# A four-layer graph network on one core: leaner neighbour lists, earlier loads of x, earlier fused weights, small first groups

## The chip, the core and the metric

One core of a Trainium2 chip runs the whole program. The metric is the device time of one execution in microseconds (us), lower being better. The kernel before takes 1764.37 us (median of three runs, 1763.55 to 1769.72). The engines are named as in the profile: PE multiplies matrices (PEld is its weight load), DVE works on vectors, ACT applies functions and copies, POOL issues the gathers and small fills, SP issues the other transfers.

## What is computed

`x` has 3327 rows of 512 numbers, and `adj` is a 3327 x 3327 matrix of zeros and ones, sparse and densest in its first rows and columns. Each of four layers computes an update from the rows that `adj` selects, adds it to `x` and normalizes each row:

```python
x = _layernorm(x + L0(x, adj, W, a1, a2))       # attention, 8 heads of 64, elu
x = _layernorm(x + L1(x, adj, ...))             # mean of all neighbours, two linear maps, relu
x = _layernorm(x + L2(x, adj, ..., 64))         # mean of the first 64 neighbours, two linear maps
x = _layernorm(x + L3(x, adj, W, a))            # attention, 4 heads of 128, elu
```

## The kernel before

**Blocks and lists.** The rows are cut into 26 blocks of 128. Block 0, the densest, is worked as a dense block. For each of the other 25 the kernel builds, on the chip, a list of its neighbours (`structure`, L863): the block of `adj` is loaded in two halves (L877, SP), ACT turns it into a 0/1 mask and adds up each row (L884), DVE multiplies the mask by column codes (L899) and draws the codes out by MAX8 and MATCH_REPLACE8 (L912 to L929). Then the per-row lists are packed into one list per block: counts go through two small matmuls that sum over the rows before (L934, L935), ACT and DVE turn the four resulting columns into start positions, negated positions and midpoints (L937 to L943), a matmul takes differences (L946), and for each run of up to ten 128-place chunks ACT makes step functions (`u`, L956), PE multiplies (L963), ACT copies out (`vc`, L966) and DVE picks indices (L971 to L984). A list is filled from the front (near columns) and from its end (far columns), so each block has one or two near runs and one far run, each worked by itself. Tiles of the pool `mid` have one buffer each, so a list's step waits for the same step of the list before.

**Prologue.** Up to L1680, 26 projections run (L1597): load a block of x, transpose it (L783), multiply by the layer-0 weights `w0` (L1048, sixteen 268-column fp32 matmuls), copy out (L1059, L1060) and store the row to the table `t0_d` that layer 0 gathers from. Before them the score columns of `w0` are made on DVE (`score_weights`, L1545 to L1548) from `a0`, which is loaded after `w0`. With each projection the list generator makes three steps (`more(3)`, L1669). `fused_weights` (L1606), begun with t = 13, multiplies the layer-1 weights together: for each of eight rows of blocks a load, four transposes, eight 512-column fp32 matmuls (L800), one copy (L1623), and at the end a bias product of 16 matmuls (L1628). One step of it is taken per projection; what is left is done by `fused.drain()` (L1680), after `g0.head` and `g0.finish` (L1678), the latter giving the last table rows. `first_rows` begins with t = 10; its scan (L1643) and the fused weights use parts of the big tile `rows`, which in the profile is called gt and which later holds the gathered rows.

**Layers.** Layers 0 to 3 take the lists in groups of up to four chunks (`groups`, L988): POOL issues one indirect gather per chunk (L1010) into a ring, and PE multiplies the gathered rows by selection matrices (L1367 in layers 0 and 3, L1844 in layers 1 and 2). `groups` has an argument `first`, the sizes of the first groups; layer 3 calls it with (1, 2), the others without. Layer 0 goes on building lists (`more(1 + k % 2)`, L1763).

**Order.** Up to layer 0's end the order of instructions on each engine is that of an automatic scheduler, which takes ready instructions by program position. After that (`manual_schedule`) it is program order. [...]

Of the kernel before, what the change touches and what calls it, by code (L numbers as in the profile page):

```python
# [8 lines left out]
F32 = mybir.dt.float32  # L9
BF16 = mybir.dt.bfloat16  # L10
# [6 lines left out]
I16 = mybir.dt.int16  # L17
# [614 lines left out]
def sparse_path(ctx, tc, flag_i, x, adj, l0_w, l0_a1, l0_a2, l1_w_self, l1_b_self, l1_w_nb, l1_b_nb,  # L632
# [67 lines left out]
    dgs = keep.tile([P, NL, 2], F32, name="dgs")  # L700
    starts = keep.tile([P, NL, 2], F32, name="starts")
    nmids = keep.tile([P, NL, 2], F32, name="nmids")
    for l in (l for ls in lists for l in ls):
        l.nmid = nmids[:, l.at]
    half = keep.tile([P, 2, NB], F32, name="half")
# [46 lines left out]
    point5 = const.tile([P, 1], F32, name="point5")  # L752
    nc.gpsimd.memset(point5, 0.5)

# [108 lines left out]
    def structure(big, mid, ps, m0):  # L863
# [26 lines left out]
        for k, b in enumerate(order):  # L890
# [7 lines left out]
            for s in range(2):  # L898
                nc.vector.tensor_mul(val[:, s * HW:(s + 1) * HW], ms[s], code[:, s * HW:(s + 1) * HW])  # L899
            nc.vector.tensor_reduce(dgs[:, b - 1, 1:2], ms[0][:, :P], AX.X, ALU.add)  # L900
            pc = ps.tile([P, 8, P], BF16, name="lp")
            nc.tensor.transpose(pc[:, 0, :], ms[0][:, :P], ident16)
            nc.scalar.activation(col0[:, b, :], pc[:, 0, :], AF.Identity, saturate=False)
            for l in lists[b]:
                L, K, cuts, a = l.L, l.K, l.cuts, l.at
                dg = dgs[:, a, 0:1]
                nc.vector.tensor_scalar(dg, half[:, 0, b:b + 1], half[:, 1, b:b + 1], 1.0, ALU.add, ALU.max)
                nc.vector.tensor_sub(dg, dg, dgs[:, a, 1:2])
                n = len(cuts) - 1
# [7 lines left out]
                cf = cand.rearrange("p s e -> p (s e)")  # L917
                sl = mid.tile([P, K + 2], F32, name="sl")
                slots = sl[:, 2:]
                for r in range(K // 8):  # L920
# [15 lines left out]
                here = mid.tile([P, 2], F32, name="here")  # L936
                nc.scalar.activation(here[:, 0:1], p1[:, 0:1], AF.Identity, bias=point5, scale=-1.0)  # L937
                nc.vector.tensor_scalar(here[:, 1:2], p1[:, 1:2], -1.0, l.room - 0.5, ALU.mult, ALU.add)
                nc.scalar.copy(starts[:, a], p1[:, 0:2])
                nc.scalar.copy(sl[:, 0:1], p1[:, 0:1])  # L940
                nc.vector.scalar_tensor_tensor(sl[:, 1:2], p1[:, 1:2], 1.0 - l.room, dg, ALU.add, ALU.subtract)
                nc.scalar.activation(l.nmid[:, 0:1], p1[:, 2:3], AF.Identity, bias=ones[:, 0:1])
                nc.vector.tensor_scalar(l.nmid[:, 1:2], p1[:, 3:4], -1.0, 1.0 - 2 * l.room, ALU.mult, ALU.add)  # L943
                yield None
                p2 = ps.tile([P, 512], F32, name="p2", tag="lp")
                nc.tensor.matmul(p2[:, :K + 2], step, sl, start=True, stop=True)  # L946
                dl = dls[a % 2]
# [3 lines left out]
                G = min(SPAN, 512 // W)  # L951
                spans = [(0, c0, l.up) for c0 in range(0, l.up, G)] + [(1, c0, L) for c0 in range(l.down, L, G)]
                for far, c0, end in spans:
                    g = min(G, end - c0)
                    u = mid.tile([P, g * P], BF16, name="u")
                    nc.scalar.activation(u, place[:, c0 * P:(c0 + g) * P], AF.Sign, bias=here[:, far:far + 1],  # L956
                                         scale=-1.0 if far else 1.0)
                    if not far:
                        yield None
                    pv = ps.tile([P, 512], F32, name="pv")  # L960
                    for c in range(g):
# [4 lines left out]
                    nc.scalar.copy(vc[:, :g * W], pv[:, :g * W])  # L966
                    if not far:
                        yield None
                    v = vc[:, :g * W].rearrange("p (c k) -> p c k", k=W)
                    off = mid.tile([P, g, 1], I16, name="off")  # L970
                    nc.vector.tensor_sub(off[:, :, 0], (npos if far else pos)[:, c0:c0 + g], v[:, :, 1 + far])  # L971
                    eq = mid.tile([P, g, K], I16, name="eq")
                    nc.vector.tensor_tensor(eq, slot[:, None, :K].to_broadcast([P, g, K]),
                                            off.to_broadcast([P, g, K]), ALU.is_equal)
                    nc.vector.tensor_mul(eq, eq, v[:, :, 3:])
                    hit = mid.tile([P, g], I16, name="hit")
                    with nc.allow_low_precision(reason="whole numbers below 4096"):
                        nc.vector.tensor_reduce(hit, eq, AX.X, ALU.add)
                    at = l.idx[:, c0:c0 + g]
                    if far:  # L980
                        nc.vector.tensor_tensor(at, at, hit, ALU.add)
                        continue
                    nc.vector.scalar_tensor_tensor(at, hit, P + 1.0, hit, ALU.is_gt, ALU.mult)
                    nc.vector.scalar_tensor_tensor(l.dst[:, c0:c0 + g], hit, P + 1.0, v[:, :, 0],  # L984
                                                   ALU.is_gt, ALU.mult)
            yield k
# [44 lines left out]
    class Gat:  # L1031
# [242 lines left out]
        def group(self, item, pools, accs, done, sall=None):  # L1274
# [22 lines left out]
            for t, k, q0, q1 in parts:  # L1297
                if q0 < q1:
                    o = t[:, q0 * P:q1 * P] if t is far else t[:, :(q1 - q0) * P]
                    nc.scalar.activation(o, place[:, (c0 + q0) * P:(c0 + q1) * P], AF.Abs,  # L1300
                                         bias=l.nmid[:, k:k + 1], scale=2.0)
            yield
# [271 lines left out]
    with ExitStack() as pro:  # L1574
# [15 lines left out]
        a0 = lent(2 * D).rearrange("p (s h o) -> p s h o", s=2, h=H0)  # L1590
        for s, src in enumerate((l0_a1, l0_a2)):
            nc.sync.dma_start(a0[:, s].rearrange("p h o -> p (h o)"), row(src, H0 * OUT0))
# [144 lines left out]
    def feed():  # L1737
# [3 lines left out]
        for n, b in enumerate(blocks):  # L1741
            if n == len(blocks) - DENSE - 2:
# [121 lines left out]
    with ExitStack() as lay:  # L1864
# [316 lines left out]
```

## Time and profile before

| what | us |
|---|---|
| median of the runs | 1764.37 |
| the profiled execution itself | 1764.85 |
| its span, first to last instruction | 1763.1 |
| first gather of layer 0 | 211.55 |
| first gather of layer 1 | 742.24 |
| first gather of layer 2 | 1133.15 |
| first gather of layer 3 | 1457.15 |

The profile has several views. The windows give, for each stretch of time, the busy time of each engine in us and its number of instructions in brackets, then PE's granted clock as a share of full speed, the share of time that the 16 transfer engines were busy, and GB/s. The groups give, for one line and shape, the count, the busy sum in us, the mean of one in ns, and the idle time of the engine just before them. The timeline lists instructions by start, with the idle time before and its releaser in square brackets. "x10" in a timeline row stands for ten instructions merged.

### The profile page before, as it was taken

What the parts mean: (1) busy time and instruction counts of PE and PEld (TensorE: products, weight loads), DVE (VectorE), ACT (ScalarE), POOL (GpSimd) and SP (SyncE); (2) the same over time, 40 slices, a digit from 0 to 9 for tenths busy, and PEclk for the clock granted to TensorE, in tenths of its full rate; (3) what the DMA queues carried; (4) which work ended last, traced back from release to release, by engine and by line L of the source; (5) the groups of instructions that cost most, each with busy time, mean ns of one, the idle gap of its engine ahead of it and who ended that gap; (6) DMA issues with size and microseconds to landing.
All of it is one profiled execution on the core that took longest, in us unless ns stands there. A gap on an engine that the chain in (4) does not pass through costs nothing.

```text
span 1763.1 us, 24351 instructions
## 1 busy us (share of the span) xinstructions
PE 1505.3 (85%) x7266; PEld 1002.5 (57%) x7266; DVE 1219.4 (69%) x3292; ACT 872.8 (50%) x2922; POOL 760.5 (43%) x909
## 2 busy tenths in 40 slices
PE   5979847889999989889999999856999973878885
PEld 4756536656666667445555554422666752767664
DVE  8989859988668788225656785537666542867897
ACT  5879645656657767312122121211444442556786
POOL 3000146555454620164444652266656206666640
PEclk9989878999999999889999999988999996979998
DMA  8787667666665542298988995387878416767761
GB/s 258 260 274 240 210 190 247 216 185 200 189 188 154 173 123 80 82 401 292 303 287 306 342 371 191 98 285 247 279 255 269 153 43 189 198 199 211 225 198 56
DMA packets 130401, 381.98 MB, mean 217 GB/s; under 512 B 22037, under 2 KB 36477, under 8 KB 130259
## 3 DMA queue, kind: packets, MB, share of 16 engines
q0 software_dynamic: 67696, 252.97, 45.2%
q1 hardware_dynamic: 62563, 127.35, 21.4%
q8 instruction: 60, 0.98, 0.2%
q14 instruction: 82, 0.67, 0.1%
HBM read 331.89 MB, written 48.37 MB: 216 GB/s over the span
## 4 chain that ended last, share of the span: by engine, by line
PE 57%; DVE 17%; ACT 9%; issue 7%; another core or an unknown queue 4%; DMA 3%; POOL 2%; SPq 0%; DVEq 0%; POOLq 0%; ACTq 0%
PE po L800 18%; PE acc L1367 10%; PE acc L1844 9%; PE po L1048 8%; PE pt L783 3%; DVE cand L912 2%; DVE gt L1348 2%; DVE gl L1348 1%; PE acc L1836 1%; DVE st L805 1%; PE acct L1477 1%; PE acc L1255 1%; ACT h L1518 1%; DVE e L1531 1%
## 5 line engine op out<-in xcount | busy, mean ns | idle before, releaser
L1010 POOL DMA_INDIRECT gt<-t_d,idx x201 | 204.0, 1015 | 369.0 <-DVE mx L1147 197.4
L1010 POOL DMA_INDIRECT gl<-t_d,idx x265 | 261.6, 987 | 185.7 <-issue 56.7
L1367 PE MATMUL acc<-gt,sel 128*128 128x264 f32 (+3 forms) x804 | 208.2, 404 | 3.4 <-issue 1.9
L800 PE MATMUL po<-wn,xt 128*128 128x512 f32 x416 | 197.5, 618 | 15.5 <-ACT xt L786 5.8
L1010 POOL DMA_INDIRECT gm<-t_d,idx x138 | 136.1, 986 | 132.7 <-PE acc L1844 79.1
L1367 PEld LDWEIGHTS acc<-gt,sel 128*128 128x128 f32 (+3 forms) x804 | 150.7, 197 | 41.0 <-issue 15.9
L1367 PE MATMUL acc<-gl,sel 128*128 128x260 f32 (+3 forms) x524 | 140.3, 412 | 14.5 <-issue 11.0
L800 PEld LDWEIGHTS po<-wn,xt 128*128 128x128 f32 x416 | 79.3, 197 | 101.8 <-issue 79.4
L1048 PE MATMUL po<-gt,xt 128*128 128x268 f32 x416 | 115.9, 424 | 15.2 <-ACT xt L790 10.9
L1348 DVE TENSOR_TENSOR gt<-gt,pg 128x1536 f32<-128x1536 f32 (+3 forms) x63 | 116.4, 1848 | 14.8 <-ACT sel L1343 12.5
L1367 PEld LDWEIGHTS acc<-gl,sel 128*128 128x128 f32 (+3 forms) x524 | 100.6, 202 | 34.7 <-issue 15.6
L1844 PE MATMUL acc<-gm,selr 128*128 128x512 f32 (+3 forms) x324 | 106.6, 452 | 5.5 <-DMA gm<-t_d,idx 5.1
L1010 POOL DMA_INDIRECT gk<-t_d,idx x65 | 67.4, 1037 | 95.5 <-DMA t_d<-mean 58.6
L912 DVE MAX8 cand<-val 128x8 f32<-128x464 uint16 (+32 forms) x184 | 107.8, 622 | 0.0
L1048 PE MATMUL po<-w,xt 128*128 128x262 f32 x416 | 98.7, 391 | 9.6 <-ACT xt L790 5.8
L786 ACT COPY xt<-pt 128x512 f32<-128x512 f32 x81 | 46.9, 587 | 119.3 <-PE pt L783 83.6
L1048 PEld LDWEIGHTS po<-gt,xt 128*128 128x128 f32 x416 | 78.6, 202 | 34.7 <-ACT xt L790 14.5
L1300 ACT ACTIVATE far<-place,nmids 128x384 int16<-128x384 int16 (+3 forms) x167 | 88.2, 544 | 13.8 <-DVE ds L1310 9.9
L1048 PEld LDWEIGHTS po<-w,xt 128*128 128x128 f32 x416 | 78.9, 192 | 27.3 <-ACT xt L790 10.0
L800 PE MATMUL po<-wx,xt 128*128 128x512 f32 x208 | 93.5, 594 | 0.0
L800 PE MATMUL po<-wl,xt 128*128 128x512 f32 x208 | 93.0, 592 | 0.0
L783 PE MATMUL pt<-s_ident,xres 128*128 128x128 f32 x500 | 78.8, 285 | 10.4 <-DVE xres L855 5.3
(377 smaller groups left out, 3268.5 us busy)
## 6 DMA issues: line engine op xcount, KB each, us to landing
ab<-in_adj_dram SPq DMA_DIRECT2D x25, 832.0 KB
ab<-in_adj_dram SPq DMA_DIRECT2D x25, 831.5 KB
t_d<-t SPq DMA_DIRECT2D x25, 512.0 KB
gm<-t_d POOLq DMA_DIRECT2D x23, 512.0 KB
t_d<-t SPq DMA_DIRECT2D x25, 384.0 KB
t_d<-tg SPq DMA_DIRECT2D x25, 264.0 KB
gd<-t_d SPq DMA_DIRECT2D x25, 264.0 KB
t_d<-tg SPq DMA_DIRECT2D x25, 260.0 KB
```

Source lines behind the costliest of these rows:

```text
L783: nc.tensor.transpose(pt[:, c, :], src[:, c * P:(c + 1) * P], ident)
L786: nc.scalar.copy(xt, pt)
L800: nc.tensor.matmul(po, xt[:, c, :], w[:, c], start=c == 0, stop=c == DC - 1)
L805: nc.vector.bn_stats(st, y)
L912: nc.vector.max(out=cand[:, s, :], in_=val[:, cuts[s]:cuts[s + 1]])
L1010: nc.gpsimd.indirect_dma_start(out=t[:m, c, :], out_offset=None, in_=table[:, :], in_offset=bass.IndirectOffsetOnAxis(ap=l.idx[:m, c0 + c: ...
L1048: nc.tensor.matmul(pw[s], xt[:, c, :], self.w[:, c, s, :], start=c == 0, stop=c == DC - 1)
L1255: nc.tensor.matmul(self.acc[h // hh][:, h % hh, :], wt[:m, h, :], G[:m, h, :], start=False, stop=False)
L1300: nc.scalar.activation(o, place[:, (c0 + q0) * P:(c0 + q1) * P], AF.Abs, bias=l.nmid[:, k:k + 1], scale=2.0)
L1348: nc.vector.tensor_mul(Gc[:, :, :OUT], Gc[:, :, :OUT], w[:, :g].rearrange("p c (h o) -> p (c h) o", o=1).to_broadcast([P, g * H, OUT]))
L1367: nc.tensor.matmul(accs[b][s], S[:m, c, :], G[:m, c, s * hh * M:(s + 1) * hh * M], start=at + c == 0, stop=last)
L1844: nc.tensor.matmul(accs[b], chosen, parts[:, k * D:(k + 1) * D], start=at + c + k == 0, stop=k == top and at + c == n - 1)
```

## The change

It has four parts.

1. **Lists.** The count of a row's ones in its first 128 columns comes from ACT (the mask of the first half is made in two ACTIVATEs, each with its own sum) and no longer from a reduction on DVE. The start positions, negations and constants come out of five small matmuls, two of them with constant rows that POOL fills per list (`rooms`: four memsets), and two ACT copies of four columns take them out; the three DVE and four ACT instructions L937 to L943 go. A far run that fits beside the last near run into ten chunks is worked with it: two `u` instructions, but one copy out, one comparison, one product, one reduction. By the sizes of the lists that holds for 22 of the 25 blocks, all but 3, 4 and 5.
2. **Loads.** `a0` is loaded ahead of `w0`; blocks 0 to 2 of x are loaded ahead of the first block of `adj`, and each projection loads the block three further on.
3. **Fused weights** begin with t = 8. At one step per projection all 17 steps then fall within the projections.
4. **First groups.** The first two groups of layers 0, 1 and 2 have one and two chunks.

The core of the diff:

```diff
-    starts = keep.tile([P, NL, 2], F32, name="starts")
-    nmids = keep.tile([P, NL, 2], F32, name="nmids")
+    sites = keep.tile([P, NL, 4], F32, name="sites")
+    starts = sites[:, :, :2]
...
+    for k, v in enumerate((0.5, -0.5, 0.0, 1.0, 0.0, 0.0, 1.0, 1.0)):
+        nc.gpsimd.memset(halves[:, k:k + 1], v)
...
-                nc.scalar.activation(m, ab[s], AF.Sign, accum_out=half[:, s, b:b + 1])
+                c0 = P if b and s == 0 else 0
+                if c0:
+                    nc.scalar.activation(m[:, :P], ab[s][:, :P], AF.Sign, accum_out=dgs[:, b - 1, 1:2])
+                nc.scalar.activation(m[:, c0:], ab[s][:, c0:], AF.Sign, accum_out=half[:, s, b:b + 1])
...
-            nc.vector.tensor_reduce(dgs[:, b - 1, 1:2], ms[0][:, :P], AX.X, ALU.add)
...
-                nc.vector.tensor_scalar(dg, half[:, 0, b:b + 1], half[:, 1, b:b + 1], 1.0, ALU.add, ALU.max)
-                nc.vector.tensor_sub(dg, dg, dgs[:, a, 1:2])
+                nc.vector.tensor_add(dg, half[:, 0, b:b + 1], half[:, 1, b:b + 1])
+                nc.vector.scalar_tensor_tensor(dg, dgs[:, a, 1:2], 0.0, dg, ALU.is_equal, ALU.max)
...
-                dg16 = mid.tile([P, 2], BF16, name="dg16")
-                nc.vector.tensor_copy(dg16, dgs[:, a])
+                dg16 = mid.tile([P, 3, 2], BF16, name="dg16")
+                nc.vector.tensor_mul(dg16, signs, dgs[:, a, None, :].to_broadcast([P, 3, 2]))
+                rooms = mid.tile([1, 8], BF16, name="rooms")
+                nc.gpsimd.memset(rooms, 0.0)
+                for c, v in ((1, l.room), (3, -l.room), (6, -2 * l.room)):
+                    nc.gpsimd.memset(rooms[:, c:c + 1], float(v))
                 p1 = ps.tile([P, 512], F32, name="p1", tag="lp")
-                nc.tensor.matmul(p1[:, 0:2], before, dg16, start=True, stop=True)
-                nc.tensor.matmul(p1[:, 2:4], middle, dg16, start=True, stop=True)
...
+                nc.tensor.matmul(p1[:, :8], ones16, halves, start=True, stop=False)
+                nc.tensor.matmul(p1[:, :8], ones16, rooms, start=False, stop=False)
+                d6 = dg16.rearrange("p k s -> p (k s)")
+                nc.tensor.matmul(p1[:, :6], before, d6, start=False, stop=False)
+                nc.tensor.matmul(p1[:, 3:4], ident16, d6[:, 0:1], start=False, stop=False)
+                nc.tensor.matmul(p1[:, 6:8], middle, d6[:, 1:3], start=False, stop=True)
+                nc.scalar.copy(sl[:, :4], p1[:, :4])
+                nc.scalar.copy(sites[:, a], p1[:, 4:8])
...
+                spans = [[(0, c0, min(G, l.up - c0))] for c0 in range(0, l.up, G)]
+                ends = [(1, c0, min(G, L - c0)) for c0 in range(l.down, L, G)]
+                if len(ends) == 1 and spans[-1][0][2] + ends[0][2] <= G:
+                    spans[-1].append(ends.pop())
...
+        a0 = lent(2 * D).rearrange("p (s h o) -> p s h o", s=2, h=H0)
+        for s, src in enumerate((l0_a1, l0_a2)):
+            nc.sync.dma_start(a0[:, s].rearrange("p h o -> p (h o)"), row(src, H0 * OUT0))
         for c in range(DC):
...
+        for b in range(3):
+            load(xres[b], x, b)
         next(made)
...
-            load(xres[b], x, b)
+            if b + 3 < NB:
+                load(xres[b + 3], x, b + 3)
...
-            if t == 13:
+            if t == 8:
                 fused.add(fused_weights())
...
-            for item in groups(pools[0], (b,), True):
+            for item in groups(pools[0], (b,), True, () if n else (1, 2)):
...
+    nc.vector.tensor_add(deg[:, 1:], deg[:, 1:], dgs[:, :, 1])
...
-        for item in groups(ring, weave):
+        for item in groups(ring, weave, first=(1, 2)):
...
-        nexts = groups(ring, weave)
+        nexts = groups(ring, weave, first=(1, 2))
```

More of the change, by code (lines that the diff above doesn't have):

```diff
@@ L700, in sparse_path @@
     dgs = keep.tile([P, NL, 2], F32, name="dgs")
-    starts = keep.tile([P, NL, 2], F32, name="starts")
-    nmids = keep.tile([P, NL, 2], F32, name="nmids")
+    sites = keep.tile([P, NL, 4], F32, name="sites")
+    starts = sites[:, :, :2]
     for l in (l for ls in lists for l in ls):
-        l.nmid = nmids[:, l.at]
+        l.nmid = [sites[:, l.at, 3:4], sites[:, l.at, 2:3]]
     half = keep.tile([P, 2, NB], F32, name="half")
@@ L751, in sparse_path @@
         nc.gpsimd.memset(dl[:, 1, 0:1], 0.0)
-    point5 = const.tile([P, 1], F32, name="point5")
-    nc.gpsimd.memset(point5, 0.5)
+    signs = const.tile([P, 3, 2], F32, name="signs")
+    nc.gpsimd.memset(signs, 1.0)
+    nc.gpsimd.memset(signs[:, 0], -1.0)
+    ones16 = const.tile([1, P], BF16, name="ones16")
+    nc.gpsimd.memset(ones16, 1.0)
+    halves = const.tile([1, 8], BF16, name="halves")
+    for k, v in enumerate((0.5, -0.5, 0.0, 1.0, 0.0, 0.0, 1.0, 1.0)):
+        nc.gpsimd.memset(halves[:, k:k + 1], v)
     H0, _, OUT0 = l0_w.shape
@@ L917, in structure @@
                 cf = cand.rearrange("p s e -> p (s e)")
-                sl = mid.tile([P, K + 2], F32, name="sl")
-                slots = sl[:, 2:]
+                sl = mid.tile([P, K + 4], F32, name="sl")
+                here, slots = sl[:, :2], sl[:, 4:]
                 for r in range(K // 8):
@@ L929, in structure @@
                 nc.vector.tensor_add(slots[:, 0:1], slots[:, 0:1], lone)
-                dg16 = mid.tile([P, 2], BF16, name="dg16")
-                nc.vector.tensor_copy(dg16, dgs[:, a])
-                p1 = ps.tile([P, 512], F32, name="p1", tag="lp")
-                nc.tensor.matmul(p1[:, 0:2], before, dg16, start=True, stop=True)
-                nc.tensor.matmul(p1[:, 2:4], middle, dg16, start=True, stop=True)
-                here = mid.tile([P, 2], F32, name="here")
-                nc.scalar.activation(here[:, 0:1], p1[:, 0:1], AF.Identity, bias=point5, scale=-1.0)
@@ L938, in structure @@
[L938 to L943, printed above, removed]
+                dg16 = mid.tile([P, 3, 2], BF16, name="dg16")
@@ L944, in structure @@
+                d6 = dg16.rearrange("p k s -> p (k s)")
[4 more added lines that the diff above has]
+                nc.scalar.copy(sites[:, a], p1[:, 4:8])
                 yield None
                 p2 = ps.tile([P, 512], F32, name="p2", tag="lp")
-                nc.tensor.matmul(p2[:, :K + 2], step, sl, start=True, stop=True)
+                nc.tensor.matmul(p2[:, :K + 2], step, sl[:, 2:], start=True, stop=True)
@@ L951, in structure @@
                 G = min(SPAN, 512 // W)
[L952 to L958, printed above, removed]
+                spans = [[(0, c0, min(G, l.up - c0))] for c0 in range(0, l.up, G)]
+                ends = [(1, c0, min(G, L - c0)) for c0 in range(l.down, L, G)]
+                if len(ends) == 1 and spans[-1][0][2] + ends[0][2] <= G:
+                    spans[-1].append(ends.pop())
+                for span in spans + [[e] for e in ends]:
+                    n, near = sum(g for _, _, g in span), not span[0][0]
+                    u = mid.tile([P, n * P], BF16, name="u")
+                    o = 0
+                    for far, c0, g in span:
+                        nc.scalar.activation(u[:, o * P:(o + g) * P], place[:, c0 * P:(c0 + g) * P], AF.Sign,
+                                             bias=here[:, far:far + 1], scale=-1.0 if far else 1.0)
+                        o += g
+                    if near:
                         yield None
                     pv = ps.tile([P, 512], F32, name="pv")
-                    for c in range(g):
+                    for c in range(n):
                         for s in range(2):
@@ L965, in structure @@
                     vc = mid.tile([P, 512], I16, name="vc")
-                    nc.scalar.copy(vc[:, :g * W], pv[:, :g * W])
-                    if not far:
+                    nc.scalar.copy(vc[:, :n * W], pv[:, :n * W])
+                    if near:
                         yield None
-                    v = vc[:, :g * W].rearrange("p (c k) -> p c k", k=W)
-                    off = mid.tile([P, g, 1], I16, name="off")
-                    nc.vector.tensor_sub(off[:, :, 0], (npos if far else pos)[:, c0:c0 + g], v[:, :, 1 + far])
@@ L972, in structure @@
-                    eq = mid.tile([P, g, K], I16, name="eq")
-                    nc.vector.tensor_tensor(eq, slot[:, None, :K].to_broadcast([P, g, K]),
-                                            off.to_broadcast([P, g, K]), ALU.is_equal)
+                    v = vc[:, :n * W].rearrange("p (c k) -> p c k", k=W)
+                    off = mid.tile([P, n, 1], I16, name="off")
+                    o = 0
+                    for far, c0, g in span:
+                        nc.vector.tensor_sub(off[:, o:o + g, 0], (npos if far else pos)[:, c0:c0 + g],
+                                             v[:, o:o + g, 1 + far])
+                        o += g
@@ L975, in structure @@
+                    eq = mid.tile([P, n, K], I16, name="eq")
+                    nc.vector.tensor_tensor(eq, slot[:, None, :K].to_broadcast([P, n, K]),
+                                            off.to_broadcast([P, n, K]), ALU.is_equal)
                     nc.vector.tensor_mul(eq, eq, v[:, :, 3:])
-                    hit = mid.tile([P, g], I16, name="hit")
+                    hit = mid.tile([P, n], I16, name="hit")
                     with nc.allow_low_precision(reason="whole numbers below 4096"):
@@ L978, in structure @@
                         nc.vector.tensor_reduce(hit, eq, AX.X, ALU.add)
[L979 to L985, printed above, removed]
+                    o = 0
@@ new lines, in structure @@
+                    for far, c0, g in span:
+                        at, h = l.idx[:, c0:c0 + g], hit[:, o:o + g]
+                        if far:
+                            nc.vector.tensor_tensor(at, at, h, ALU.add)
+                        else:
+                            nc.vector.scalar_tensor_tensor(at, h, P + 1.0, h, ALU.is_gt, ALU.mult)
+                            nc.vector.scalar_tensor_tensor(l.dst[:, c0:c0 + g], h, P + 1.0, v[:, o:o + g, 0],
+                                                           ALU.is_gt, ALU.mult)
+                        o += g
@@ L1300, in group @@
                     nc.scalar.activation(o, place[:, (c0 + q0) * P:(c0 + q1) * P], AF.Abs,
-                                         bias=l.nmid[:, k:k + 1], scale=2.0)
+                                         bias=l.nmid[k], scale=2.0)
             yield
@@ L1589, in sparse_path @@
                                   l0_w[s * H0 // 2:(s + 1) * H0 // 2, c * P:(c + 1) * P, :].rearrange("h p o -> p h o"))
-        a0 = lent(2 * D).rearrange("p (s h o) -> p s h o", s=2, h=H0)
-        for s, src in enumerate((l0_a1, l0_a2)):
-            nc.sync.dma_start(a0[:, s].rearrange("p h o -> p (h o)"), row(src, H0 * OUT0))
         g0 = Gat("g0", t0_d, H0, OUT0, w0, 0)
+        for b in range(3):
+            load(xres[b], x, b)
         next(made)
```

## The prediction

> **What bounds the kernel now.** I began with the page's engine totals: PE is busy 85% of the span, DVE 69%. An average over five stages decides nothing, so I cut the part that the change touches (0 to 420 us, and the starts of layers 1 and 2) into windows.
>
> ```profile
> core 0: us, PE busy (x) PEld busy (x) DVE busy (x) ACT busy (x) POOL busy (x), PEclk, DMA share, GB/s
> ...
> 50.00:110.00 60.00, 49.27 (x346) 36.90 (x345) 59.45 (x268) 52.66 (x187) 0.00 (x0) 0.92 0.80 262
> 110.00:160.00 50.00, 46.68 (x295) 32.45 (x293) 42.34 (x168) 42.56 (x147) 0.00 (x0) 0.96 0.73 248
> 160.00:205.00 45.00, 41.67 (x251) 29.57 (x249) 43.50 (x185) 40.14 (x140) 0.00 (x0) 0.96 0.75 241
> 205.00:226.00 21.00, 18.48 (x55) 9.54 (x55) 11.22 (x59) 6.11 (x16) 11.10 (x12) 0.84 0.63 175
> 226.00:244.00 18.00, 1.06 (x13) 0.98 (x14) 2.63 (x12) 2.93 (x8) 10.29 (x11) 0.62 0.63 182
> 244.00:262.00 18.00, 10.85 (x78) 8.68 (x76) 16.39 (x57) 14.03 (x39) 4.34 (x5) 0.72 0.58 197
> 262.00:340.00 78.00, 63.30 (x348) 48.21 (x347) 69.55 (x211) 46.08 (x131) 45.71 (x49) 0.89 0.70 220
> 340.00:420.00 80.00, 71.15 (x350) 47.16 (x349) 72.26 (x241) 49.14 (x152) 45.56 (x45) 0.96 0.66 203
> 420.00:700.00 280.00, 263.38 (x1369) 187.78 (x1369) 214.50 (x468) 192.23 (x684) 117.10 (x129) 1.00 0.52 157
> ```
>
> In the prologue (to 205) PE is 92 to 93% busy from 110 on and DVE is as full, so neither can take work for nothing. From 205 to 244 both stand largely idle. From 262 to 420, where lists are still built, DVE is 90% and PE 85% busy. After 420 PE is 94% busy: what has been gained by then is passed on to the end. The timeline tells what the hole at 205 to 244 is made of.
>
> ```profile
> 210.24 8.53 PE L800 MATMUL po<-gt,xt 128*128 128x512 f32 x16
> 211.55 1.56 POOL L1010 DMA_INDIRECT gt<-t_d,idx  x1 [197.41 <-DVE mx L1147]
> 218.61 7.03 PE L1628 MATMUL po<-gt,bb 128*128 128x512 f32 x16
> 234.50 0.27 ACT L966 CAST vc<-pv 128x135 int16<-128x135 f32 x1 [9.32 <-remote]
> 242.97 0.20 ACT L966 CAST vc<-pv 128x54 int16<-128x54 f32 x1 [6.57 <-remote]
> ```
>
> Two causes lie behind one another: to 226 PE runs fused weights left over, then ACT waits 9.3 and 6.6 us for something the profile can't name, while POOL sends its opening burst of gathers.
>
> [...] From the two sizes of L973 below, the slope is 93/96 = 0.97 ns and the fixed part 204 − 48 × 0.97 = 157[...]
>
> **Lists.** Groups by form, up to 210 us; after the bar, sum in us and mean in ns:
>
> ```profile
> L900 DVE TENSOR_REDUCE dgs<-m 128x1 f32<-128x128 bf16 x18 | 5.0, 278 | 0.0
> L941 DVE SCALAR_TENSOR_TENSOR sl<-p,dgs 128x1 f32<-128x1 f32 x16 | 2.5, 153 | 0.0
> L938 DVE TENSOR_SCALAR here<-p 128x1 f32<-128x1 f32 x16 | 2.4, 152 | 0.0
> L943 DVE TENSOR_SCALAR nmids<-p 128x1 f32<-128x1 f32 x16 | 2.4, 149 | 0.0
> L973 DVE TENSOR_TENSOR eq<-slot,off 128x144 int16<-128x144 int16 x5 | 1.5, 297 | 0.0
> L973 DVE TENSOR_TENSOR eq<-slot,off 128x48 int16<-128x48 int16 x5 | 1.0, 204 | 0.0
> ```
>
> DVE loses four instructions per list, 278 + 153 + 152 + 149 = 0.73 us busy. In a full queue instructions overlap: the timeline has L941 at 207.06, L900 at 207.13, L1089 at 207.32, so they cost 0.07 and 0.19; with 0.07 for the other two that is 0.40 us. A merged run saves the fixed parts of one comparison, product and reduction: 0.157 + 0.155 + 0.148 by the same sum, 0.46 busy, 0.22 after three overlaps of 0.08. The prologue makes about 17 lists, some 14 merged: 17 × 0.40 + 14 × 0.22 = 9.9 us. If DVE takes over some copies of projections from ACT, I guess 2.5 are lost: 7.4. Eight lists in layer 0 save 8 × 0.62 = 5.0. L932 and the cast are only exchanged for the like: 0.
>
> ACT loses L937 to L940 (0.27 + 0.28 + 0.17 + 0.18) and one `vc` copy (0.20) and gains two copies (0.36), a second ACTIVATE [...] and its sum read-out (0.21): −0.3 us, hidden, as ACT is 80 to 90% busy. PE gets five small matmuls for two, 0.03 each: 25 × 0.1 = 2.5 us in all. POOL gets four memsets, at 0.04 to 0.09 (its small fills in the trace) 0.16 to 0.36 us a list; in the prologue POOL is idle (0.00), in layer 0 see rival D.
>
> **Loads.** PE waited for x only 0.8 us in all (L783), as the scheduler had hoisted x's loads already. `a0` goes ahead of eight issues of `w0`, 0.54 us each, so 4.3 us earlier; DVE stood 5.8 us for it:
>
> ```profile
> 10.78 0.69 DVE L1545 TENSOR_TENSOR pr<-gt 128x512 f32<-128x512 f32 x1 [5.78 <-DMA gt<-in_L_gnn_a_dram]
> ```
>
> Against it, the first block of `adj` stands behind three blocks of x on SP's queue, 0.79 MB at 273 GB/s (16 to 50), 2.9 us. I take −2, range −5 (all of a0's wait and more of the start) to +5 (the lists start late and DVE, full from 50 to 110, never makes it up).
>
> **Fused weights.** Left behind the head are 2 of 8 rows: transposes 1.97 (L783), 8.53 (L800), and the bias 7.03 (L1628), about 17.5 us. They go among the projections. PE's idle time there is 60 − 49.27 = 10.7 (50 to 110) and 95 − 46.68 − 41.67 = 6.7 (110 to 205), 17.4 against 17.5 + 2.5 of small matmuls: not all of it can be used. I put the last projection 2 us later, paid by the start's −2: the first gather stays at 211.5 ± 5. The loads and transposes begin five projections of 7 us, 35 us, earlier, on SP ahead of later `adj` blocks; the bytes are the same, 0. The scan's fill of `rows` on POOL (L1641) shrinks, hidden: 0.
>
> **The boundary.** With PE free after the head, DVE can go on with lists: its idle time in 205 to 226 is 21 − 11.22 = 9.8, of which I take 8 as filled. Leaner lists in layer 0 give 2.5 of 5.0, as PE at 85% binds half the time. DVE's slack in the prologue pulls in more of the list work: 4 of 7.4. The extra group in layer 0 costs its fixed evictions, +1 (0 to 2).
>
> Sum: −2 + 2 − 8 − 2.5 − 4 + 1 = −13.5. A cap: PE's idle time in 262 to 420 is 158 − 134.45 = 23.5, so there is room. From the profiled execution's own 1764.85 (span 1763.1 + 1.75): 1751.35; the median is 0.5 lower: **1751**.
>
> **First groups of layers 1 and 2.**
>
> ```profile
> 745.00:785.00 40.00, 33.81 (x91) 17.02 (x90) 6.73 (x16) 6.03 (x11) 25.15 (x29) 0.83 1.02 403
> ...
> 1120.00:1205.00 85.00, 52.65 (x173) 21.88 (x173) 40.71 (x86) 11.51 (x27) 49.46 (x49) 0.82 0.72 236
> ```
>
> In layer 1 the transfers are full (1.02, 403 GB/s): when the first chunk is handed on doesn't matter. In layer 2 PE is busy with blocks' own parts (L800) from 1132.09 to 1145.99 and goes straight on to gathered rows. Both 0 ± 2; if the own parts were not there, layer 2 would gain up to two chunks' gathers, 2 × 1.25 = 2.5.
>
> **The rivals.**
>
> A, as summed: 1744 to 1758 for its own range (boundary 4 to 9.8, pull-in 0 to 6, loads ± 3).
>
> B, the second hole goes too. A first group of one chunk lets PE begin while the burst is running, and ACT is no longer held at 225 and 236. DVE's idle time in 226 to 244 is 18 − 2.63 = 15.4 more: 1751 − 15 = 1736. For it: the hole begins where PE turns to gathered rows. Against: it ends near the burst's end (about 239), and layer 3, which has first groups of one and two chunks already, shows the same wait:
>
> ```profile
> 1485.52 0.18 DVE L1337 TENSOR_TENSOR sc<-pg,gk 128x16 f32<-128x16 f32 x1 [10.32 <-remote]
> ```
>
> C, no cover. PE's idle time in the prologue is short waits in order, not room; the 20 us of fused and small matmuls move the first gather about 10 us later, and only what lists save is left: 1751 + 11 = 1762. For it: 93% busy. Against: from 50 to 110 PE waits for DVE, not the reverse.
>
> D, slower: POOL. The four memsets of a list stand on POOL's queue among gathers that wait for free buffers; a gather takes 1.25 us there, a group of four 5.0. PE's matmul with `rooms` then waits, and behind it on PE, in order, all of layer 0. POOL already waited for PE at this place:
>
> ```profile
> POOL gt L1010 <- PE acc L1367: 24.6, 21, 3.5
> ```
>
> (sum in us, count, mean). A wait of 5.0 with 2.5 hidden, in each of 8 lists, is 20; less the 8 that remain of the gain, +12: 1764.4 + 12 = 1776. It decides from 12/8 = 1.5 us per list. Against: the scheduler may place the fills early, as they depend on no data, though with one buffer only after the list before.
>
> **Chances and range.** A 0.45, B 0.20, C 0.22, D 0.13. What this kernel's measurement tells from no change is about 0.5%, 8.8 us: faster is under 1755.6, slower over 1773.2. A lies to 0.40 below that and 0.05 within; B is faster; C 0.01 faster, 0.21 within; D slower. Faster 0.61, same 0.26, slower 0.13. The range leaves out B's lower quarter to third and D's upper half, 0.06 each: 1731 to 1774.
>
> **What would show it.** Fused: L800 x16 and L1628 before the last L1048, nothing of them after; the first gather at 211.5 ± 5 (A, B), about 221 (C). Boundary: DVE idle in the 20 us after the head under 4. B: ACT's waits of 9.3 and 6.6 us gone and the clock after them at 0.9. Lists: L900, L937 to L943 gone, the last list done about 15 us before 415. D: PE waiting for POOL's memsets, over 1.5 us each. Layers 1 to 3: lengths (391, 324, 306 us between first gathers) within 2 us. I am wrong in kind if those lengths move by more, or if PE waits for POOL.

## The result, and the profile after

The changed kernel takes 1776.1 us (median of 18 runs, 1765.06 to 1782.8), the kernel before 1767.3 us in as many: ratio 1.0039, 95% interval 1.0023 to 1.0056. By the ratio it is slower by some 7 us (0.39%); 1751 was forecast. The profiled execution took 1779.75 us (span 1778.0), so this pair of profiles shows 15 us where the runs show 7.

| from, to | before, us | after, us | difference |
|---|---|---|---|
| start to first gather of layer 0 | 211.5 | 228.2 | +16.7 |
| layer 0 | 530.7 | 519.8 | −10.9 |
| layer 1 | 390.9 | 397.7 | +6.8 |
| layer 2 | 324.0 | 324.2 | +0.2 |
| layer 3 | 305.9 | 307.9 | +2.0 |

The windows of the kernel after, cut as those shown of before, and two more: 219.4 to 240.4 lies to the first gather as 205 to 226 did before, and the last line has the 20 us from the first gather on:

```profile
core 0: us, PE busy (x) PEld busy (x) DVE busy (x) ACT busy (x) POOL busy (x), PEclk, DMA share, GB/s
...
50.00:110.00 60.00, 47.55 (x358) 33.99 (x357) 57.65 (x241) 49.38 (x161) 1.52 (x24) 0.91 0.76 261
110.00:160.00 50.00, 48.06 (x305) 34.92 (x303) 41.34 (x139) 45.34 (x149) 1.01 (x16) 0.97 0.79 264
160.00:205.00 45.00, 44.87 (x250) 30.12 (x251) 33.24 (x124) 30.31 (x116) 0.76 (x12) 1.00 0.52 174
205.00:226.00 21.00, 14.67 (x101) 11.64 (x100) 14.96 (x60) 17.40 (x59) 0.78 (x12) 0.93 0.59 194
226.00:244.00 18.00, 7.13 (x56) 5.73 (x56) 15.43 (x63) 11.34 (x31) 12.43 (x12) 0.51 0.77 249
244.00:262.00 18.00, 0.60 (x3) 0.19 (x1) 0.90 (x7) 2.79 (x8) 11.22 (x12) 0.58 0.74 241
262.00:340.00 78.00, 61.99 (x347) 47.05 (x347) 67.12 (x190) 42.08 (x122) 46.28 (x63) 0.83 0.67 211
340.00:420.00 80.00, 72.53 (x365) 48.93 (x362) 69.85 (x206) 48.39 (x140) 42.54 (x57) 0.96 0.67 206
420.00:700.00 280.00, 262.75 (x1371) 187.82 (x1370) 214.15 (x475) 193.37 (x684) 122.86 (x135) 1.00 0.53 161
...
219.40:240.40 21.00, 5.72 (x62) 4.92 (x63) 19.86 (x84) 16.46 (x43) 10.01 (x13) 0.59 0.78 250
228.20:248.20 20.00, 7.68 (x57) 5.87 (x56) 14.09 (x52) 12.00 (x34) 15.71 (x15) 0.59 0.84 287
```

The 20 us from the first gather on in the kernel before:

```profile
211.55:231.55 20.00, 14.33 (x41) 6.12 (x40) 6.42 (x27) 2.83 (x6) 15.43 (x16) 0.93 0.69 189
```

From 160 to 205 PE has almost no idle time left (44.87 of 45), while DVE and ACT are freer than before (33 and 30 us, against 43 and 40). The first gather has moved, so the hole behind the head is compared by its distance from it: from 219.4 to 240.4 DVE is busy for 19.86 of 21 us, before for 11.22, and in the 20 us from the gather on for 14.09, before for 6.42. The first part of the hole is largely filled. The second part has moved with the gathers to 244 to 262, where nearly everything stands. The timeline, with the matmuls in question and the waits:

```profile
196.71 7.03 PE L1654 MATMUL po<-gt,bb 128*128 128x512 f32 x16
...
214.66 3.88 PE L1071 MATMUL po<-gt,xt 128*128 128x268 f32 x16
...
228.22 2.33 POOL L1033 DMA_INDIRECT gt<-t_d,idx  x1 [2.99 <-DVE dg L940]
...
252.19 0.59 ACT L1366 CAST sel<-pg 128x512 f32<-128x512 bf16 x1 [5.44 <-remote]
261.96 0.36 DVE L1359 TENSOR_REDUCE sc<-pg 128x64 f32<-128x192 f32 x1 [16.34 <-remote]
```

The bias product (L1654, before L1628) now lies ahead of the last projection (L1071, before L1048), as was meant, and the first gather comes 16.7 us later. Where from is read by cutting each prologue at 110 us. It is counted from the first projection's first matmul to 3.4 us after the last one's end (called the end of the projections below). Before:

```profile
18.00:110.00 92.00, 77.75 (x491) 59.12 (x491) 91.35 (x349) 75.42 (x273) 0.00 (x0) 0.93 0.81 266
110.00:207.50 97.50, 88.63 (x545) 62.11 (x543) 88.33 (x364) 84.28 (x289) 0.00 (x0) 0.96 0.75 245
```

After:

```profile
12.50:110.00 97.50, 77.74 (x498) 56.24 (x497) 91.47 (x317) 72.44 (x247) 1.77 (x28) 0.93 0.77 260
110.00:221.90 111.90, 106.57 (x647) 75.78 (x644) 85.69 (x305) 90.29 (x318) 2.28 (x36) 0.98 0.64 213
```

PE starts 5.5 us earlier, yet has been busy for the same 77.7 us by 110: the early start is idle time (19.8 us, before 14.3). After 110 it has 17.9 us more to do and hides 3.5 of them (idle 5.3, before 8.9). The projections thus end 17.9 − 3.5 = 14.4 us later, and the head after them takes 2.3 us longer.

### The profile page after: what moved, and what is told of

It is laid out like the page before. It is cut to its first block, busy times and chain, and to the rows that moved or that the text cites. A ratio compares the mean times of both kernels' runs of the same rounds, so it can differ in the third digit from the quotient of the medians.

```text
span 1778.0 us, 24415 instructions
## 1 busy us (share of the span) xinstructions
PE 1512.0 (85%) x7341; PEld 1008.5 (57%) x7341; DVE 1204.4 (68%) x3136; ACT 868.4 (49%) x2903; POOL 764.6 (43%) x1018
## 4 chain that ended last, share of the span: by engine, by line
PE 63%; DVE 12%; ACT 8%; issue 7%; DMA 4%; another core or an unknown queue 3%; POOL 2%; SPq 0%; DVEq 0%; ACTq 0%; POOLq 0%
PE po L806 20%; PE acc L1390 14%; PE acc L1871 9%; PE po L1071 9%; PE pt L789 3%; PE acc L1863 1%; ACT m L893 1%; PE acc L1278 1%; PE acct L1500 1%; DMA ab<-in_adj_dram 1%; DVE gt L1371 1%; DVE cand L920 1%; DVE gl L1371 1%; ACT h L1541 1%
## 5 line engine op out<-in xcount | busy, mean ns | idle before, releaser
L1033 POOL DMA_INDIRECT gm<-t_d,idx x140 | 139.9, 999 | 144.7 <-PE acc L1871 93.1
L1071 PE MATMUL po<-gt,xt 128*128 128x268 f32 x416 | 116.0, 422 | 15.6 <-ACT g0fall L1083 8.2
L1371 DVE TENSOR_TENSOR gt<-gt,pg 128x1536 f32<-128x1536 f32 (+3 forms) x64 | 116.6, 1822 | 18.1 <-ACT sel L1366 13.3
L1871 PE MATMUL acc<-gm,selr 128*128 128x512 f32 (+3 forms) x324 | 110.9, 464 | 7.1 <-DMA gm<-t_d,idx 4.4
L1071 PE MATMUL po<-w,xt 128*128 128x262 f32 x416 | 97.2, 386 | 11.6 <-ACT xt L796 8.8
L1323 ACT ACTIVATE far<-place,sites 128x128 int16<-128x128 int16 (+3 forms) x167 | 87.9, 543 | 27.7 <-DVE ds L1331 10.9
L1071 PEld LDWEIGHTS po<-gt,xt 128*128 128x128 f32 x416 | 78.5, 201 | 35.4 <-ACT g0fall L1083 9.1
L1071 PEld LDWEIGHTS po<-w,xt 128*128 128x128 f32 x416 | 78.0, 190 | 28.4 <-ACT xt L796 14.5
```

What stands on the lines that cost most here:

```text
L1033: nc.gpsimd.indirect_dma_start(out=t[:m, c, :], out_offset=None, in_=table[:, :], in_offset=bass.IndirectOffsetOnAxis(ap=l.idx[:m, c0 + c: ...
L1071: nc.tensor.matmul(pw[s], xt[:, c, :], self.w[:, c, s, :], start=c == 0, stop=c == DC - 1)
L1371: nc.vector.tensor_mul(Gc[:, :, :OUT], Gc[:, :, :OUT], w[:, :g].rearrange("p c (h o) -> p (c h) o", o=1).to_broadcast([P, g * H, OUT]))
L1871: nc.tensor.matmul(accs[b], chosen, parts[:, k * D:(k + 1) * D], start=at + c + k == 0, stop=k == top and at + c == n - 1)
```

## The experiments

They ran in five batches, on chips that the record numbers 3 (e1 to e4), 10 (c0 to c3), 7 (d0, e5, e6, n1), 6 (h1, h2) and 14 (s1, s2). On all five the kernel before takes 1674 to 1677 us, 5% less than in the runs above. The record doesn't number the chip of those; it is called the first one below, and that it is yet another is the author's guess from the 5%. Each is compared by its ratio to the kernel before in the same batch; a difference of 0.01 in a ratio is called a point. Times in the table are of each one's profile, in us: the first projection, PE's busy time from there to 110 and its idle time from 110 to the end of the projections, the first gather, the lengths of layers 0 and 1. Each is from one profile. The changed kernel's order up to the first gather was profiled three times (the first profile, c0 and e5), with the first gather at 228.2, 233.9 and 228.7, so differences of less than some 5 us in that column say little.

| kernel | first proj. | busy to 110 | idle after | first gather | layer 0 | layer 1 | ratio (95%) |
|---|---|---|---|---|---|---|---|
| before (d0_before) | 18.0 | 77.1 | 9.0 | 212.2 | 506.8 | 391.0 | 0.9995 (0.9978 to 1.0012) |
| changed (c0_after) | 13.1 | 77.5 | 6.6 | 233.9 | 487.8 | 393.5 | 0.9994 (0.9979 to 1.0009) |
| e5_old_first | 12.5 | 77.6 | 5.5 | 228.7 | 489.5 | 390.9 | 1.0016 (1.0005 to 1.0028) |
| e3_old_lists | 12.4 | 78.7 | 8.2 | 232.3 | 493.3 | 392.3 | 1.0041 (1.0025 to 1.0057) |
| e1_fused13 | 15.3 | 79.2 | 14.2 | 224.2 | 495.8 | 393.8 | 1.0008 (0.9996 to 1.0020) |
| e2_fused17 | 15.3 | 78.9 | 10.9 | 208.2 | 503.1 | 393.0 | 0.9954 (0.9935 to 0.9973) |
| e4_old_loads | 18.5 | 79.4 | 3.8 | 219.7 | 486.2 | 393.7 | 0.9954 (0.9936 to 0.9972) |
| c1_old_a0 | 14.3 | 80.1 | 5.0 | 220.8 | 489.8 | 394.0 | 0.9962 (0.9949 to 0.9975) |
| c2_old_x | 16.9 | 77.8 | 5.9 | 224.8 | 484.8 | 394.0 | 0.9986 (0.9976 to 0.9996) |
| c3_old_loads_fused17 | 18.1 | 81.7 | 13.3 | 209.6 | 506.1 | 394.0 | 0.9976 (0.9965 to 0.9986) |
| e6_lists_only | 18.6 | 76.7 | 8.3 | 214.2 | 499.7 | 391.6 | 0.9945 (0.9928 to 0.9963) |
| n1_no_bias | 12.4 | 77.9 | 5.8 | 222.3 | 488.0 | 393.2 | 0.9969 (0.9959 to 0.9980) |
| h1_copies_first | 12.5 | 78.8 | 6.4 | 227.6 | 488.1 | 394.2 | 1.0005 (0.9991 to 1.0018) |
| s1_scan_later | 12.5 | 77.7 | 4.2 | 228.6 | 483.3 | 393.0 | 0.9994 (0.9980 to 1.0007) |
| s2_lists_scan_later | 18.2 | 78.1 | 4.5 | 209.9 | 491.2 | 390.9 | 0.9933 (0.9912 to 0.9954) |

**One part undone.** The fused weights later:

```diff
-            if t == 8:
+            if t == 13:
```

> The changed kernel with the fused weights begun with t = 13 again, the other three parts kept. Theory P (the prologue is bound by PE, none of the moved fused work was hidden): the last projection and the first gather come 14 to 15 us earlier, first gather at 212 to 215 us instead of 228.2; the 17.5 us of fused work are back behind the head, under POOL's opening burst, so layer 0 gets some 7 us longer; net about 7 us faster than the changed kernel, ratio to the kernel before 0.998 to 1.002. Rival L (the new list steps, with five small matmuls and POOL's constants, hold up the prologue): first gather still at 220 or later, ratio about 1.003. Rival F (small first groups cost it in layers 1 and 2): first gather 212 to 215 but ratio still 1.002 to 1.004.

> The changed kernel with the fused weights begun with t = 17: four of eight rows and the bias, about 30 us of PE work, behind the head. Theory P: first gather another 11 to 13 us earlier than with t = 13, at about 201; the opening burst of gathers lasts some 30 us from there and covers the 30 us of PE work; 5 to 10 us faster than with t = 13, ratio 0.993 to 0.998. Rival (nothing is covered by the burst, work behind the head costs as much as work ahead of it): total as with t = 13, within 3 us. Rival L: first gather barely moves.

With t = 13 the ratio lies in the range of theory P, but the first gather is 9 us later than it allows (224.2): something else than the fused work holds the prologue. Nor did the 7 us come that P has as the gain over the changed kernel: that kernel had 0.9994 in its own batch (c0, below), this one 1.0008. With t = 17 the first gather comes another 16 us earlier, layer 0 gets 7.3 us longer, and the ratio is below those of the kernel before and the changed one: work behind the head is about half covered. The lists as before (their hunks of the diff taken back):

> The kernel before with the changed loads, fused weights from t = 8 and small first groups; the lists are built as before. Theory P: first gather at 227 to 232 us, as the fused work is still in the prologue; layer 0 about 3 us longer than in the changed kernel; ratio 1.004 to 1.008. Rival L: first gather at 212 to 218 and ratio about 1.000, since the list steps were the cause.

It came nearly as P has it: 232.3 and 1.0041. Rival L falls. The loads as before (`a0` after `w0`, each x block with its own projection):

```diff
-        for b in range(3):
-            load(xres[b], x, b)
...
-            if b + 3 < NB:
-                load(xres[b + 3], x, b + 3)
+            load(xres[b], x, b)
```

> The changed kernel with a0 behind w0 and each block of x loaded with its own projection, as before. Theory P: the first projection starts at about 18 us instead of 12.5, and the first gather comes 3 to 6 us later, at 231 to 234; ratio 1.005 to 1.008. Rival D (the new order of loads delays the first lists and stalls PE at 40 to 60 us, where its busy time fell from 18.5 to 10.7 of 20 us): that stall goes and the first gather comes no later, or earlier, than 228; ratio 1.000 to 1.003.

P is wrong here, and this is the main find: without the earlier loads the first projection starts 6 us later and the first gather comes 9 us *earlier* (219.7, against 228.7 in e5, whose prologue is that of the changed kernel; 14 us against c0). The stall that rival D names is gone (PE idle before 64 us: 4.7 in e4, 13.1 in e5), but late first lists are not its reason: the first is done at 44.6 us in e4 and at 44.4 in e5. PE's matmuls of projections (L1071) alone show where the start is lost. In e4, then in e5:

```profile
8.00:64.00 56.00, 34.81 (x128) 0.97 0.84 288
8.00:110.00 102.00, 58.39 (x202) 0.95 0.81 269
...
8.00:64.00 56.00, 32.50 (x100) 0.91 0.80 264
8.00:110.00 102.00, 55.13 (x184) 0.93 0.77 261
```

Of the 416 such matmuls (16 to a projection) PE has done 28 fewer by 64 us with the early start, and 18 fewer by 110. Then the halves of this part, beside the changed kernel again; c1 moves only the `a0` loads back, c2 only those of x:

> The changed kernel itself once more, beside the parts of it, to have its profile and ratio from the same chip: ratio 1.002 to 1.006; first gather near 228 us and the pause of PE between 40 and 62 us as in its first profile.

> The changed kernel with only the order of a0 and w0 as before; x is still loaded three blocks ahead. Undoing both gave 0.9954. Theory X (loading x ahead is what costs: PE runs ahead of the first lists and the queues are then ordered so that it waits for them at 40 to 62 us): ratio stays at 1.002 to 1.006, first gather 226 to 232. Rival A (a0 ahead of w0 is what costs): ratio 0.994 to 0.998, first gather near 219.

> The changed kernel with only the loads of x as before; a0 is still ahead of w0. Theory X: ratio 0.993 to 0.997, first gather 216 to 220, PE's pause at 40 to 62 us under 4 us. Rival A: ratio 1.002 to 1.006.

Theory X falls: c1 came as rival A has it, while c2 fits neither (0.9986, 224.8). `a0`'s place costs 0.32 points at either setting of x (0.9962 to 0.9994, and 0.9954 to 0.9986), x ahead 0.08 points, which is within the noise. In this batch the changed kernel is level with the one before (0.9994); it was expected to be slower, as it was on the first chip. With loads as before and t = 17 together:

> The changed kernel with the loads as before and the fused weights begun with t = 17: lean lists, small first groups, and some 30 us of fused work behind the head. If the two effects add (loads back: 0.9954 against 1.0039; t = 17: 0.9954 against 1.0039), ratio 0.986 to 0.990 and first gather at 195 to 202. If the two are one effect, since both only take a pause out of the same stretch of the prologue, ratio 0.993 to 0.996 and first gather at 205 to 210.

Neither: 0.9976 is worse than each alone, at the edge of the noise. With the loads as before t = 8 is better than t = 17, with the new ones worse. The effects don't add: with t = 17 the early loads bring no later first gather (208.2 with them, 209.6 without) and no higher ratio (0.9954, against 0.9976).

**One part alone, and doses.** The kernel before for its profile; the small first groups undone (`first=()` in layers 0, 1 and 2); the lists alone:

> The kernel before itself, to have its profile beside those of the other variants on such a chip: ratio 1.000; first gather at 211 to 218, about 39 us of idle PE before the last projection is done, layer 1 between 390 and 395 us.

> The changed kernel with the first groups as before (up to four chunks) in layers 0, 1 and 2. Theory: the small first groups are worth 0 within 3 us in sum, since the opening pause while POOL issues its first gathers stays either way and layers 1 and 2 begin with own parts: ratio within 0.002 of the changed kernel's (0.998 to 1.004), layer 1 within 2 us of 393. Rival F (they cost layer 1 the 6.8 us by which it was longer in the first profile): ratio 0.004 lower than the changed kernel's, layer 1 5 us or more shorter.

> The kernel before with the new lists alone. Theory: they leave the prologue as long as it was (first gather 207 to 214, since PE and the fixed number of list steps per projection set its length, not DVE) and shorten layer 0 by 4 to 6 us; ratio 0.995 to 0.999. Rival L or D (the small matmuls and POOL's constants hold up PE): ratio 1.001 or more.

The lists are the only part that ran alone, and they pay: the first gather hardly moves (+2.0), layer 0 is 7.1 us shorter, ratio 0.9945. Layer 1 is 390.9 to 391.6 us in all five profiles of these batches with the old first groups and 392.3 to 394.2 in all eleven with the new: they cost it some 2.5 us, between the theory and rival F, while the runs (1.0016, against 0.9994 in another batch) make the whole kernel rather faster with them. A dose of PE work, leaving out the loop of the bias product (layer 1's bias is then incomplete):

> The changed kernel without the bias product of the fused weights (16 matmuls, 7.0 us of PE, and their copies), so that layer 1's bias is left incomplete. It is a dose of PE work taken out of the prologue. Theory P (PE is the bound there, work costs its own length): first gather 5 to 9 us earlier than in the changed kernel, ratio about 0.004 lower. Rival (PE's idle time of some 25 us in the prologue is room, and something else sets the length): first gather within 2 us, ratio within 0.0015.

7.0 us of PE less, first gather 6.4 us earlier than in e5 (11.6 than in c0), ratio 0.0025 lower than the changed kernel's, that is 4 us: in this order PE's work after 110 us costs about its length at the first gather.

**What the earlier loads run into.** ACT's timeline in the changed kernel (c0) shows the two copies of one projection's half (L1082, L1083) apart, with list work between:

```profile
52.44 0.41 ACT L1082 COPY tg<-po 128x264 f32<-128x264 f32 x1
52.71 1.40 ACT L971 ACTIVATE u<-place,sl 128x1280 bf16<-128x1280 int16 x1
53.98 0.61 ACT L982 CAST vc<-pv 128x510 int16<-128x510 f32 x1
54.44 0.35 ACT L892 ACTIVATE m<-ab 128x128 bf16<-128x128 int32 x1
...
54.74 1.51 ACT L893 ACTIVATE m<-ab 128x1536 bf16<-128x1536 int32 x1
...
56.21 0.20 ACT L1083 COPY g0fall<-po 128x8 f32<-128x8 f32 x1
```

PE's waits in that stretch of it (sum in us, count, longest):

```profile
PE po L1071 <- ACT g0fall L1083: 5.3, 2, 5.0
PE p L956 <- DVE sl L937: 3.5, 1, 3.5
```

In c1 each pair stands together. So the copies were given precedence in the scheduler's order:

```diff
+                with tc.high_priority() if self.k == 0 else nullcontext():
                     nc.scalar.copy(tb[:, s * hh:(s + 1) * hh, :], by_head[:, :, 1:])
...
```

> The changed kernel, complete, with one thing added: the two copies of a projection's half out of PSUM are given precedence over list work when ACT's order is written. In the changed kernel such a pair stands apart at 52 to 56 us, with list work of 3.5 us between, and PE waits 5.0 us for the second. Theory Q (with a0 and x early, the order on ACT puts list work ahead of copies that PE needs, and that is what the earlier loads cost): that wait is gone, first gather at 216 to 224 instead of 228 to 234, ratio 0.993 to 0.997. Rival R (the lists' own pace sets the prologue, the wait only shows it): PE waits for something else by as much, first gather at 226 or later, ratio 0.998 or more.

> The new lists alone, with the same precedence for the copies. If the place of the copies limits the prologue in general, the first gather comes before 210 and the ratio falls below 0.993; if only the order that came with the earlier loads was unlucky, first gather 211 to 216 and ratio 0.993 to 0.997 as without it.

PE's waits before 64 us in h1:

```profile
PE po L1071 <- ACT xt L796: 4.9, 5, 1.6
PE p L956 <- DVE sl L937: 3.8, 1, 3.8
PE po L1071 <- issue: 2.0, 1, 2.0
```

The 5.0 us wait is gone, and others stand in its place (those for `xt` had been 0.7 us): 12.5 us of idle time before 64, in c0 12.4; first gather 227.6, ratio 1.0005. Theory Q falls, a tempting line of the profile with it. The scheduler dealt other work anew as well: in h1 the first list is done at 32.6 us, not 44. h2 is as without it (213.9, layer 0 499.8, ratio 0.9953 with 0.9937 to 0.9970). Then DVE's scan was taken out of the middle of the first list:

```diff
+            with tc.issue_after(marks[-1].ins):
                 nc.vector.tensor_tensor_scan(so_far, m0, m0, 0.0, ALU.add, ALU.bypass)
```

(`marks` collects each list's L936; the product after the scan likewise.)

> The changed kernel, complete, with DVE's scan of the first rows (7.1 us) and the product after it (3.6 us) put behind the sixth and the eighth list instead of in the middle of the first. Theory O (the opening is set by DVE's work on the first lists, so that PE's earlier start only makes it wait): first list done at 33 to 37 us instead of 44, PE idle before 64 us 4 to 8 us instead of 13, first gather at 219 to 225, ratio 0.994 to 0.998. Rival (DVE's 10.7 us are only paid later, or PE waits for something else as in the run with the copies first): first gather at 226 to 231, ratio 0.998 to 1.002.

> The new lists alone with the same scan put later. With loads as before PE starts at 18 us and had only 4.7 us of idle time before 64 us, so theory O expects little here: first gather 209 to 214, ratio 0.992 to 0.996. The rival expects the same as without it, 0.993 to 0.997.

The windows of s1 to 64, to 110 and after:

```profile
12.40:64.00 51.60, 43.38 (x254) 33.01 (x253) 44.55 (x162) 41.94 (x151) 0.77 (x12) 0.97 0.82 282
64.00:110.00 46.00, 34.39 (x218) 22.68 (x217) 42.23 (x149) 28.19 (x92) 1.02 (x16) 0.78 0.65 225
...
110.00:221.20 111.20, 107.05 (x672) 75.96 (x670) 89.84 (x310) 92.58 (x325) 2.30 (x36) 1.00 0.65 220
```

The first list is done at 32.4 instead of 44 us and PE has been busy for 43.4 us by 64 (e5: 38.4), as theory O has it. But by 110 it stands at 77.7 again, with 180 matmuls of projections done, and the first gather at 228.6. The rival's numbers came. s2 is the fastest version run (0.9933, faster than the kernel before and the changed one); against the lists alone (0.9945), in another batch, the intervals overlap.

## Why the prediction was wrong

**The step that failed** is "the first gather stays at 211.5 ± 5", the sum of −2 for the loads and +2 for fused work hidden in PE's idle time. It came 16.7 us later. In the order d0, e6, e4, e5 it grew by 2.0 us with the lists, 5.5 with the fused weights (and first groups, which come later), 9.0 with the loads: 16.5. Each step is the difference of two profiles that may be some 5 us off, and in another order the shares would differ: with t = 17 the loads have none.

**Loads: −2 was written, with −5 to +5; it is +9 in the first gather, and 0.4 points of the ratio** (e4 0.9954, changed 0.9994), that is 6.7 us. The start was rightly seen to come earlier, by 5 to 6 us. Why that should bring the end forward was never argued. In all the profiles, 15 in the table and the two first, PE has been busy for 76.7 to 81.7 us by 110, whether it began at 12.4 or at 18.6, with lean lists or old, with copies first or the scan later. The order on PE mixes list steps with projections, three per projection, and the seventh list is done between 104 and 116 us in every profile. That the lists set the pace fits this, but is argued: no run brought that list clearly earlier. An earlier start is waited away, and with t = 8 more than that. Equal busy time is not equal work: by the two lines to 110 above, a projection's matmul took 0.289 us on average in e4, at a granted clock of 0.95, and 0.300 in e5, at 0.93. So e5 is 18 matmuls of projections behind e4 at 110, 4.7 us at the 0.26 us that one takes there later. In busy time the loss, e4 to e5, reads as 1.8 us less by 110, 5.4 us more for the same matmuls in all (the granted clock to 110 is 0.94 in e4, 0.93 in e5; after 110, 1.00 and 0.98) and 1.7 us more idle time. Why `a0`'s place does most of it stays open: two mechanisms that the profile offered, the split copies and the scan, were taken away and gave nothing back. A third, transfers that come later behind the early loads, has little room: from the first projection to 205 us PE, DVE and ACT wait 4.3 us for transfers in the first profile and 1.4 in c0.

**Fused weights: the cover was not there.** The working counted PE's idle 10.7 us of 50 to 110 and 6.7 after as room. The first was not room here: 12.4 us are idle there in the changed kernel too, 60 − 47.55, and fused matmuls took the place of projections (by 110 us 184 of their matmuls are done, before 224). Rival C said this ("short waits in order, not room") and gave it 10 us and 0.22. Moved with the first groups but without the loads (e6 to e4), the fused work cost 5.5 us ahead of the first gather, and layer 0 got 13.5 shorter; the ratio doesn't show the difference (0.9945, 0.9954).

**The boundary: right in kind.** −8 for DVE's idle time, −2.5 and −4 for lists, +1 for the group (the author's guess, which no run isolates) make −13.5 in layer 0; measured −10.9 on the first chip, −17.3 (e5) and −19.0 (c0) on the others. "DVE idle in the 20 us after the head under 4" held where the working had counted (219.4 to 240.4: 21 − 19.86 = 1.1 us, before 9.8); in the 20 us from the first gather on it is 5.9, before 13.6. The lists alone gave 9 us (0.9945), of which the 6.5 they were given is within the interval. Their last one is then done 5.7 us earlier (d0, then e6):

```profile
L928 DVE TENSOR_SCALAR lone<-cnt x25: 134/144/273, 44.3 to 394.2; 128x1 f32<-128x1 f32 x25
...
L936 DVE TENSOR_SCALAR lone<-cnt x25: 129/146/155, 44.0 to 388.5; 128x1 f32<-128x1 f32 x25
```

In the changed kernel it comes at 417.5 us, before at 415.5, where 15 us earlier was forecast: what the lists gain, the later first gather takes. Their prices held in the trace: L952 169 ns, L953 187, the split mask's read-out 214, its second ACTIVATE 225 (332 and 1497 for the two, against 1604 for a half done in one), the fill of `rooms` 94 and 92.

**The second hole: rival B wrong, but its place moved.** On the first chip the waits "remote" came back behind the new first gather (16.3 and 5.4 us): the hole ends 34 us after the first gather, before 31.5. There the fused work had lain under it in part. In c0 and e5 there are no such waits, and layer 0 gained 6 to 8 us more from being rid of the fused work. That this makes the difference between 1.0039 and 0.9994 is argued, not shown; no experiment ran on the first chip.

**Rival D** did not come: in the changed kernel's first profile PE never waits for `rooms`, in c0 once, 4.8 us. The fills wait for PE instead (17 waits, 208.7 us of POOL's idle time before 228), which costs nothing as POOL has no other work there: from 12.5 to 221.9 us all its 64 instructions, 4.06 us, are these fills. The prediction misread one line here: the third number of such a line is the longest wait, not the mean, so POOL's 21 waits for PE took 24.6/21 = 1.2 us on average, not 3.5.

**Layers 1 to 3: "0 ± 2" each was too small for layer 1.** Of the 6.8 us, 1.9 are a pause that no other profile has, with slower matmuls after it (the timeline of the kernel after; eight such take 3.60 elsewhere):

```profile
867.63 3.60 PE L806 MATMUL po<-wl,xt 128*128 128x512 f32 x8
...
874.49 5.40 PE L806 MATMUL po<-wx,xt 128*128 128x512 f32 x8 [1.90 <-issue]
```

Together 3.7; the other 3.1 are near the 2.5 that the small groups cost on the other chips.

**The form of the sum** was wrong too: it added terms of one schedule. The scheduler can write another order for an edit: e1, where only t differs, begins its projections at 15.3 us, not at 12.5. And effects of 4 to 7 us changed sign with what stood beside them (t = 17 against t = 8: −0.40 points with the new loads, +0.22 with the old).

## What to carry to other kernels

Idle time of an engine is room only where that engine itself is not waiting for steps that come at another's pace (here PE's 10.7 us from 50 to 110 became 12.4 with fused work put there): cut the stage where the bound changes, and ask of each piece whether more work or an earlier start would shift its end. A start that comes earlier ahead of such a stretch can be worth nothing or less (6 us earlier, and the first gather 9.0 later), and work moved into a full stretch can cost about its length (6.4 us at the first gather for the 7.0 of the bias product), however idle the engine looks on average. Measure progress by what an engine has done (202 matmuls of projections by 110 us in e4, 184 in e5), not by how long it was busy (79.4 and 77.6 us). Where an automatic scheduler deals the order, test the parts of a change one by one and keep those that pay alone: here the lists did, and with the other three the gain was gone.

## What the runs showed that was not expected

The same kernel before takes 1767 us on the first chip and 1675 on the five others. The waits named "remote" sum to 137 us over PE, DVE, ACT and POOL in the first profile (136 in the changed kernel's) and to 1.8 and 0 in d0 and c0; in d0 layers 0, 2 and 3 are 24, 24 and 43 us shorter, layer 1 is not (391.0, before 390.9). Whether the chip itself or something that ran beside the core makes these waits, no run tells. And with the order up to the first gather unchanged, that gather came at 228.7 (e5) and at 233.9 (c0): PE's granted clock to 110 us was 0.93 in one and 0.86 in the other.
